# A four-layer WKV and graph-convolution kernel: both ends rearranged, three groups of rows for 1/std, maxima of three tiles per operation, square of means from PSUM

## The chip, the cores and the metric

The kernel runs on one core of a Trainium2 chip. The core has five engines, each with its own stream of instructions: TensorE (PE in the profile; its weight loads are shown as PEld) multiplies matrices into PSUM, VectorE (DVE) does arithmetic between tensors, ScalarE (ACT) does functions of one operand, GpSimd (POOL) does arithmetic between tensors too, and SyncE (SP) issues most transfers. They meet at semaphores. The metric is the time of one execution on the device in microseconds.

## What is computed

The input x has 16 images of 192 channels and 56 x 56 points in float32. Three layers of one kind and a fourth of another kind follow each other, each adding to x what it computes from the group-normalized x:

```python
def rwkv(x):                      # layers 0, 1, 2, on tokens t = 0..3135
    k, v, r = x @ Wk.T, x @ Wv.T, x @ Wr.T
    h = sigmoid(r) * 0.5 * (wkv_scan(w, u, k, v) + flip(wkv_scan(w, u, flip(k), flip(v))))
    h = (h - mean(h)) * rsqrt(var(h) + 1e-5) * ln_g + ln_b      # over the 192 channels
    return h @ Wo.T
def graph_conv(x):                # layer 3
    xj = maximum(0, roll(x, +-2, rows) - x, roll(x, +-2, columns) - x)
    return gelu(batch_norm(concat(x, xj) @ conv_w.T + conv_b))
for l in range(3):
    x = x + rwkv(group_norm(x))   # 32 groups of 6 channels, over all points
x = x + graph_conv(group_norm(x))
```

The scan is a recurrence over tokens with a decay for each channel; it runs forward and backward, so that a layer needs all tokens of an image before its backward half ends, and the group norm needs all of them before the next layer begins.

## The kernel before

**Tiling.** Images go in eight pairs. The 384 channels of a pair lie in three tiles of 128 rows: j = 0 has channels 0 to 127 of the first image, j = 2 those of the second, and the middle tile j = 1 has the last 64 channels of both, the first image's in rows 0 to 63 (LO in the code), the second's in rows 64 to 127 (HI). The 3136 tokens are cut into NL = 7 chunks of L = 448, eight rows of the image each. All x and h tiles are 128 x 3 x 448, so one operation over all three j has 1344 elements in a row.

**Runs and units.** A run is one layer of one pair: 8 x 4 runs. A run of layers 0 to 2 has seven A units (keys, values, forward scan of a chunk; a_keys to a_y) and seven B units, from chunk 6 down to 0 (backward scan, gate, norm over channels, output projection, residual; b_gate to b_stats). A run of layer 3 has seven C units (c_rows to c_add). Chunks of x go through DRAM between the runs (b_x stores, load_chunk loads).

**Steps.** Two chains of pairs run against each other: while one pair is in its backward half, the other is in its forward half or its convolution. The list of steps (L1215 to L1270) pairs units: 102 steps have a B and an A unit, 66 an A alone, 42 a B and a C, 24 a B alone, 14 a C alone, one none. The order of every engine's instructions is the order in which the step functions (both_a, both_a_first, both_c, forward_a, forward_c, backward_alone) call the parts; the whole of it stands under manual_schedule (L1707), so no scheduler moves anything.

**Norm.** The group norm isn't applied to x. Sums and sums of squares of each chunk are taken on ACT (chunk_stats, L730 to L735: an Identity and a Square for each of the three j, each with an accumulated output into `junk`). For the eight first-layer runs they are taken from the input (Z units); for later layers in b_stats. norm_sums (L738) reduces them on DVE (L740) and multiplies by a group matrix into the PSUM bank psg; norm_var (L746) makes nm, the negative mean, its square m2 (L751), the variance (L753) and 1/std; norm_fold multiplies the weights by it. The mean is carried as one more column of the chunk's tile (mean_column, L764), which a projection turns into a bias. For a run of layer 3 that column sits in chunk 0, so its product has L + 1 columns (c_product, L1131) and gives the bias that c_gelu (L1140) uses for all chunks. For the very first run, all seven chunks are loaded and `count` takes their statistics (L1712, L1713) before anything else of the run.

**1/std of the norm over channels.** For each chunk of a B unit: b_squares (ACT, L1040) squares h; b_sums (PE, L1047, L1049) puts into one bank `st` four bands of 32 rows, two with sums and two with sums of squares, one of each for the two images; b_rs1 (ACT, L1055) and b_rs2 (PE, L1059) subtract the squared mean. b_rs3 then makes 1/std as exp(-0.5 ln) in rows 64 to 127 of the tile `rs`, the first image's in rows 64 to 95, the second's in 96 to 127. b_spread (PE, L1071) copies them by a product with the selection matrix `pick` onto the rows of the three tiles: six instructions, two for each j, with 32 rows of `rs` for j = 0 and 2 and 64 rows for j = 1. b_scale (DVE, L1076) multiplies h by it, b_out (PE, L598 to L607, tile ops) projects, and b_x (DVE, L1089) adds to x. The weight operand is called `fpicks` in the profile. The core of it:

```python
        S.activation(rs[HI, :], st[HI, :L], AF.Ln, bias=eps4[HI, :])      # b_rs3, L1063
        release(st)
        S.activation(rs[HI, :], rs[HI, :], AF.Exp, scale=-0.5)            # L1065
...
        for j, rows in ((0, slice(64, 96)), (2, slice(96, P)), (1, HI)):  # b_spread, L1070
            PE.matmul(ps[j][:, :L], pick[rows, j, :], rs[rows, :], start=True, stop=True)
```

**Convolution.** c_rows (L1108) takes the maximum of the two row neighbours: most of a chunk from the chunk itself (L1114), the first and the last two image rows against 112 tokens of the chunk before and after, which were loaded into the tile (L1115, L1116). c_columns (L1118) takes the column neighbours for each j with one large operation and two for the edges (L1125, L1126, L1127), then the maximum with x (L1128) and with the row maxima (L1129). c_product multiplies x (half 0) and the maxima (half 1) into the same banks (cv), c_gelu applies bias, scale and gelu on ACT (L1150; the gelu needs another table of functions, L1155 loads the first back), c_add adds x on POOL (L1159), and store() sends a unit's result in four transfers one step later.

**The end.** Step 239 is the last with a B unit: chunk 0 of pair 7's layer 2, beside chunk 5 of pair 6's convolution. Steps 240 and 241 have that convolution's chunk 6 and nothing else new, and steps 242 to 248 the seven C units of pair 7 in the order 0 to 6. After the schedule a flag is set on DVE from all the checks of value ranges; where a check fails, a general path (L75 to L470) computes everything again. It isn't taken here.

Of the kernel before, what the change touches and what calls it, by code (L numbers as in the profile page):

```python
# [34 lines left out]
F32 = mybir.dt.float32  # L35
# [438 lines left out]
def fast_path(ctx: ExitStack, tc: tile.TileContext, flag, x, wproj, wfold, wcfold, wconst, wgroup, sums, picks, vecs, out):  # L474
# [237 lines left out]
    class Run:  # L712
        def __init__(self, pr, l, stats, src=None, first=None):
            self.pr, self.l, self.stats, self.src = pr, l, stats, src
            self.xa, self.xb, self.xz = {}, {}, {}
            if first is not None:
                self.xa[0] = first
            self.begun, self.before = False, None
            self.bias, self.ps = {}, {}
            self.ek, self.ekv, self.h, self.den, self.sg, self.rs = {}, {}, {}, {}, {}, {}  # L720
            self.m, self.ml, self.q, self.p = {}, {}, {}, {}
            self.done = set()
# [23 lines left out]
    def norm_var(run):  # L746
        m = run.ps["g"][:, 0:6].rearrange("p (j s) -> p j s", s=2)
        nm = run.nm = stile("nm")
        V.tensor_scalar(nm, m[:, :, 0:1], -1.0 / T, None, ALU.mult)
        m2 = stile("m2")  # L750
        V.tensor_mul(m2, nm, nm)  # L751
        var = run.var = stile("var")
        V.scalar_tensor_tensor(var, m[:, :, 1:2], 1.0 / T, m2, ALU.mult, ALU.subtract)  # L753
        release(run.ps.pop("g"))
        V.tensor_scalar(var, var, EPS, None, ALU.add)
        rstd = run.rstd = stile("rstd")
        S.activation(rstd, var, AF.Ln)
        S.activation(rstd, rstd, AF.Exp, scale=-0.5)
        run.chk = small.tile([P, NCHK], F32, tag="chk", name=name("chk"))
        mean_check = run.chk[:, 3 * NL + 9 : NCHK].rearrange("p (j o) -> p j o", o=1)  # L760
        V.scalar_tensor_tensor(mean_check, var, -MEAN_MAX, m2, ALU.mult, ALU.add)
        mean_column(run, run.xa[0])
# [47 lines left out]
    def load_weights(run):  # L810
        kv = wpool.tile([P, 2, FCOLS], F32, tag="kv", name=name("wkv"))
        if run.l == NLAYERS:
            nc.sync.dma_start(kv, wcfold)
            run.weights = kv, None
        else:
            nc.sync.dma_start(kv, wfold[run.l, :, 0:2, :])
            r = wpool.tile([P, 1, FCOLS], F32, tag="r", name=name("wr"))
            nc.sync.dma_start(r, wfold[run.l, :, 2:3, :])
            run.weights = kv, r
        load_ahead(("C" if run.l == NLAYERS else "A", run, 0))  # L820
# [14 lines left out]
    def load_ahead(unit):  # L835
# [7 lines left out]
        if kind == "C" and c not in run.xb:  # L843
# [217 lines left out]
    def b_rs3(run, c):  # L1061
        rs, st = run.rs[c], run.ps["st"]
        S.activation(rs[HI, :], st[HI, :L], AF.Ln, bias=eps4[HI, :])  # L1063
        release(st)
        S.activation(rs[HI, :], rs[HI, :], AF.Exp, scale=-0.5)  # L1065

    def b_spread(run, c):
        rs = run.rs.pop(c)
        ps = run.ps["rsb"] = banks("rsb")
        for j, rows in ((0, slice(64, 96)), (2, slice(96, P)), (1, HI)):  # L1070
            PE.matmul(ps[j][:, :L], pick[rows, j, :], rs[rows, :], start=True, stop=True)  # L1071
# [36 lines left out]
    def c_rows(run, c):  # L1108
# [3 lines left out]
        if c == 0:  # L1112
            mean_column(run, m)
        V.tensor_max(m.t[:, :, SHIFT:E], xt[:, :, 0 : E - SHIFT], xt[:, :, 2 * SHIFT : L])  # L1114
        V.tensor_max(m.t[:, :, 0:SHIFT], m.t[:, :, 0:SHIFT], xt[:, :, SHIFT : 2 * SHIFT])  # L1115
        V.tensor_max(m.t[:, :, E:L], xt[:, :, E - SHIFT : E], m.t[:, :, E:L])  # L1116

    def c_columns(run, c):  # L1118
# [3 lines left out]
        for j in ORDER:  # L1122
            xr = xt[:, j, :].rearrange("p (r w) -> p r w", w=W)
            mr = ml.t[:, j, :].rearrange("p (r w) -> p r w", w=W)
            V.tensor_max(mr[:, :, 2 : W - 2], xr[:, :, 0 : W - 4], xr[:, :, 4:W])  # L1125
            V.tensor_max(mr[:, :, 0:2], xr[:, :, W - 2 : W], xr[:, :, 2:4])  # L1126
            V.tensor_max(mr[:, :, W - 2 : W], xr[:, :, W - 4 : W - 2], xr[:, :, 0:2])  # L1127
        V.tensor_max(ml.t, ml.t, xt)  # L1128
        V.tensor_max(m, m, ml.t)  # L1129

    def c_product(run, c, half):  # L1131
        n = L + 1 if c == 0 else L
# [7 lines left out]
    def c_gelu(run, c, more):  # L1140
        g, ps = run.ml[c], run.ps["c"]
        if c == 0:
# [22 lines left out]
    def c_end(run, c, more):  # L1165
        c_gelu(run, c, more)
        c_add(run, c)

# [25 lines left out]
    for pr in range(npairs):  # L1194
        runs = [Run(pr, 0, None)]
        for l in range(NLAYERS):
            runs[-1].follow = Run(pr, l + 1, None)
            runs[-1].follow.before = runs[-1]
            runs[-1].dst = [dram.tile([P, 3, L], F32, tag=f"x{pr}_{l}_{c}", name=name("xd")) for c in range(NL)]
            runs.append(runs[-1].follow)  # L1200
# [11 lines left out]
    while ready[turn] is not None:  # L1212
# [16 lines left out]
        if len(streams) == 1 or ready[other] is None:  # L1229
# [8 lines left out]
            else:  # L1238
                ready[turn] = None
            steps += [[None, None, []]] + [[None, u, []] for u in units]  # L1240
# [367 lines left out]
    def forward_c(a, nback, nfront):  # L1608
# [5 lines left out]
        if h and ahead and nfront[0] == "A":  # L1614
# [16 lines left out]
            return  # L1631
        c_product(*a, 0)
        c_rows(*a)
        c_columns(*a)
# [12 lines left out]
        c_end(*a, nfront is not None and nfront[0] == "C")  # L1647
# [58 lines left out]

    with tc.manual_schedule(engines={PE.engine, V.engine, S.engine, G.engine, nc.sync.engine}):  # L1707
        S.preload_act_table_set(TABLES)
        first = chains[0][0]
        for c in range(NL):  # L1710
            load_ahead(("Z", first, c))
        for c in range(NL):  # L1712
            count([(first, c, j) for j in ORDER], 3)  # L1713
        for i, (b, f, z) in enumerate(steps):
# [32 lines left out]
            elif f:  # L1747
                forward_c(f[1:], nback, nfront)
# [7 lines left out]


    least = small.tile([P, 1], F32, tag="p2", name="fleast")
    V.tensor_reduce(least, ok, mybir.AxisListType.X, ALU.min)
    ps = bank("psok")  # L1760

    PE.matmul(ps[0:32, 0:1], ones[:, 0, :], least, start=True, stop=True)
    V.tensor_scalar(flag, ps[0:1, 0:1], (P - 0.5) / C, None, ALU.is_lt)
# [44 lines left out]
def _lay_out(inputs):  # L1808
# [24 lines left out]
    picks[64, 0, :] = picks[64, 1, 0:64] = picks[96, 1, 64:P] = picks[96, 2, :] = 1.0  # L1833
# [22 lines left out]
```

## Time and profile before

| quantity | value |
|---|---|
| median of 3 executions | 5122.39 us (5105.55 to 5124.11) |
| the profiled execution | 5118.31 us |
| its span in the profile | 5116.5 us |
| granted TensorE clock, mean | 0.95 |
| HBM | 324.83 MB read, 154.14 MB written, 94 GB/s |
| the chain that ended last, largest lines | POOL L1033 6%, L1032 6%, L1031 5%; DVE scan L875 p 5%, q 4% |
| largest groups | DVE scans L875, two groups of 1008: 1023.5 and 1020.1 us |

The profile shows one execution. A group of instructions has a line of the kernel, an engine, the tiles it writes and reads, a shape, a count, the busy time and the mean of one, and the idle time of the engine just before, with what ended it. The chain that ended last is followed back from the last instruction: at each step to what released it, or else to the instruction before it on its engine. POOL and DVE durations of one operation differ from one instance to the next where both engines are busy, so undisturbed durations are read from instances with no neighbour. The slices of the page show DVE at 5 tenths in the first slice and 5 in the last, 8 or 9 in almost all others; the first and the last 128 us have less work side by side than the rest.

### The profile page before, as it was taken

How to read it: one execution, taken by the hardware profiler on the slowest of the kernel's cores; microseconds unless marked ns; L12 is line 12 of the kernel's file. 1: busy time of each engine (PE TensorE's matmuls, PEld its weight loads, DVE VectorE, ACT ScalarE, POOL GpSimd, SP SyncE). 2: the span in 40 equal slices, each digit the busy share in tenths (PEclk: the TensorE clock that was granted, in tenths of full speed). 3: DMA queues.
4: the chain of work that ended last, by engine and by line, in shares of the span. 5: the costliest groups of instructions: out<-in, count | busy, mean ns of one | idle time of the engine just before them, and what ended most of it. 6: DMA issues, size and time to landing. Idle time of an engine off the chain costs nothing.

```text
span 5116.5 us, 51926 instructions
## 1 busy us (share of the span) xinstructions
PE 4664.1 (91%) x15542; PEld 1474.9 (29%) x15542; DVE 4769.5 (93%) x6275; ACT 3690.8 (72%) x7163; POOL 2898.8 (57%) x2247
## 2 busy tenths in 40 slices
PE   7899999999898999999989899999989999999897
PEld 3222222222222223222323222322222322223222
DVE  5999999998999999999899999999989999999995
ACT  6777777776767777777776777777767577777672
POOL 1656656654455666565455556666635466566562
PEclk9999999999899999999999999999999999999998
DMA  6122222234242222223424222222343322222233
GB/s 173 60 84 82 80 87 84 79 103 144 79 129 88 85 76 89 78 76 121 138 89 126 79 83 72 89 89 78 114 124 113 103 65 84 78 71 89 74 100 119
DMA packets 314276, 482.49 MB, mean 94 GB/s; under 512 B 66432, under 2 KB 306688, under 8 KB 313984
## 3 DMA queue, kind: packets, MB, share of 16 engines
q1 hardware_dynamic: 312832, 477.59, 29.2%
q8 instruction: 126, 2.06, 0.2%
q10 hardware_dynamic: 1152, 1.48, 0.1%
q14 instruction: 166, 1.36, 0.1%
HBM read 324.83 MB, written 154.14 MB: 94 GB/s over the span
## 4 chain that ended last, share of the span: by engine, by line
PE 35%; DVE 23%; POOL 18%; ACT 17%; issue 4%; DMA 2%; SPq 1%; POOLq 0%; DVEq 0%; ACTq 0%
POOL p L1033 6%; POOL p L1032 6%; POOL ekv L1031 5%; DVE p L875 5%; DVE q L875 4%; PE st L1049 3%; DVE q L890 2%; ACT sg L1003 2%; PE st L1059 2%; ACT sg L978 2%; ACT ek L978 2%; PE rsb L1071 2%; PE r L598 2%; PE r L605 2%; PE r L600 2%
## 5 line engine op out<-in xcount | busy, mean ns | idle before, releaser
L875 DVE TENSOR_TENSOR_SCAN q<-fdecays,ek 128x449 f32<-128x449 f32 (+1 forms) x1008 | 1023.5, 1068 | 12.8 <-ACT ek L920 10.3
L875 DVE TENSOR_TENSOR_SCAN p<-fdecays,ekv 128x449 f32<-128x449 f32 (+1 forms) x1008 | 1020.1, 1064 | 15.1 <-ACT ek L884 14.9
L1031 POOL TENSOR_TENSOR ekv<-ekv,ek 128x448 f32<-128x448 f32 x504 | 609.6, 1210 | 607.6 <-ACT ek L978 284.3
L982 POOL TENSOR_TENSOR p<-p,q 128x1344 f32<-128x1344 f32 x168 | 512.2, 3049 | 749.8 <-ACT q L978 468.6
L1033 POOL TENSOR_TENSOR p<-p,sg 128x448 f32<-128x448 f32 x504 | 616.8, 1224 | 83.4 <-ACT sg L978 34.0
L1032 POOL TENSOR_TENSOR p<-p,ekv 128x448 f32<-128x448 f32 x504 | 602.3, 1195 | 39.5
L886 POOL COPY ekv<-p 128x3 f32<-128x3 f32 x282 | 243.8, 864 | 567.0 <-DVE p L875 544.4
L920 ACT ACTIVATE ek<-k,k 128x448 f32<-128x448 f32 x504 | 297.1, 632 | 285.6 <-PE k L601 229.2
L1040 ACT ACTIVATE ek<-p 128x448 f32<-128x448 f32 x504 | 286.3, 572 | 231.2 <-POOL p L1033 230.8
L735 ACT ACTIVATE fjunk<-x 128x448 f32<-128x448 f32 x672 | 387.7, 577 | 37.6 <-DVE x L1089 11.1
L1071 PE MATMUL rsb<-rs,fpicks 32*128 32x448 f32 (+1 forms) x1008 | 355.3, 619 | 43.1 <-ACT rs L1065 43.1
L1076 DVE TENSOR_TENSOR p<-p,rsb 128x448 f32<-128x448 f32 x504 | 281.4, 611 | 103.7 <-PE rsb L1071 103.7
L890 DVE SCALAR_TENSOR_TENSOR ek<-ek,fcc,q 128x896 f32<-128x896 f32 x336 | 377.7, 1163 | 0.0
L734 ACT ACTIVATE fjunk<-x 128x448 f32<-128x448 f32 x600 | 343.5, 572 | 13.6
L1089 DVE SCALAR_TENSOR_TENSOR x<-ops,fwob,x 128x448 f32<-128x448 f32 x504 | 313.2, 669 | 29.5 <-PE ops L601 16.2
L890 DVE SCALAR_TENSOR_TENSOR q<-ek,fcc,q 128x896 f32<-128x896 f32 x336 | 334.7, 1035 | 6.3 <-ACT cvb L954 4.6
L940 DVE SCALAR_TENSOR_TENSOR ekv<-v,v,ek 128x448 f32<-128x448 f32 x504 | 312.3, 671 | 15.3 <-PE v L601 10.9
L890 DVE SCALAR_TENSOR_TENSOR ekv<-ekv,fcc,p 128x896 f32<-128x896 f32 x336 | 321.7, 997 | 0.0
L996 ACT ACTIVATE sg<-r,r 128x448 f32<-128x448 f32 x504 | 312.4, 626 | 10.2 <-PE r L607 8.3
L890 DVE SCALAR_TENSOR_TENSOR p<-ekv,fcc,p 128x896 f32<-128x896 f32 x336 | 293.6, 913 | 3.8 <-POOL ekv L886 1.7
L975 ACT ACTIVATE q<-q 128x1344 f32<-128x1344 f32 x168 | 221.5, 1318 | 96.9 <-DVE q L890 87.8
L598 PE MATMUL ops<-p,fwo 128*128 128x448 f32 x336 | 206.1, 700 | 84.5 <-DVE p L1076 84.5
(235 smaller groups left out, 11485.2 us busy)
## 6 DMA issues: line engine op xcount, KB each, us to landing
x<-xd SPq DMA_DIRECT2D x240, 672.0 KB, 5.3
xd<-x SPq DMA_DIRECT2D x168, 672.0 KB, 3.9
x<-in_x_dram SPq DMA_DIRECT2D x320, 224.0 KB, 4.5
x<-in_x_dram SPq DMA_DIRECT2D x320, 112.0 KB, 4.4
out_dram<-ml SPq DMA_DIRECT2D x112, 224.0 KB, 2.3
m<-xd SPq DMA_DIRECT2D x112, 168.0 KB, 5.2
wkv<-in_wfold_dram SPq DMA_DIRECT2D x24, 640.0 KB, 5.5
out_dram<-ml SPq DMA_DIRECT2D x112, 112.0 KB, 2.3
```

Of the source, the lines that this page charges most:

```text
L734: S.activation(junk, xt[:, j, :], AF.Identity, accum_out=stats[:, 0, j, c : c + 1])
L735: S.activation(junk, xt[:, j, :], AF.Square, accum_out=stats[:, 1, j, c : c + 1])
L875: V.tensor_tensor_scan(out, dec[:, column(j)].to_broadcast([P, L if first else L + 1]), e, 0.0, ALU.mult, ALU.add)
L890: by_channel(lambda js, i: V.scalar_tensor_tensor(dst.t[:, js, :], e.t[:, js, :], cc[:, i : i + 1], state.t[:, js, :], ALU.mult, ALU.add))
L940: V.scalar_tensor_tensor(e.t[:, j, :], ps[j][:, 0:L], b[:, j, :], run.ek[c].t[:, j, :], ALU.add, ALU.mult)
L982: G.tensor_mul(run.h[c].t, run.h[c].t, den.t)
L996: S.activation(sg.t[:, j, :], ps[j][:, 0:L], AF.Exp, bias=b[:, j, :], scale=-1.0, accum_out=run.chk[:, at : at + 1])
L1031: G.tensor_mul(y.t[:, j, :], y.t[:, j, :], den.t[:, j, :])
L1032: G.tensor_add(h.t[:, j, :], h.t[:, j, :], y.t[:, j, :])
L1033: G.tensor_mul(h.t[:, j, :], h.t[:, j, :], sg.t[:, j, :])
L1071: PE.matmul(ps[j][:, :L], pick[rows, j, :], rs[rows, :], start=True, stop=True)
L1089: V.scalar_tensor_tensor(xj, ps[j][:, 0:L], wob[:, column(j)], xj, ALU.add, ALU.add, accum_out=run.new[:, 0, j, c : c + 1] if c == 0 else ...
```

## The change

It has five parts.

1. The first run's sums are taken on DVE, one reduction for a whole chunk; ACT keeps only the squares.
2. m2 is computed by scalar_tensor_tensor from the mean in PSUM and nm, in place of a product of nm with itself.
3. b_rs3 writes 1/std a second time, into rows 0 to 63 of `rs`, by another Exp. The middle tile's matmul of b_spread takes these rows, and `pick` is laid out for it: 32 rows from 64, 32 from 96, 64 from 0.
4. The two edge operations of c_rows become one over a strided view, and c_columns treats the three tiles together: three operations in place of nine.
5. The last run's C units go in the order 3, 4, 5, 2, 6, 1, 0; unit c0 = 3 carries the mean's column and the bias. The step of the last C unit of the run before is written out anew (`final` in forward_c): the squares of the last backward chunk are issued first, the row and column maxima of unit 3 stand ahead of the scaling on DVE, those of unit 4 ahead of and behind the residual, the second half of the product and the gelu come last. The very last unit goes tile by tile, with gelu, an addition on DVE and the transfers for each tile, and the range flag is set before it. The other steps of the list are unchanged.

```diff
-            self.begun, self.before = False, None
+            self.begun, self.before, self.nm = False, None, None
+
+            self.c0 = 0
...
-        V.tensor_mul(m2, nm, nm)
+        V.scalar_tensor_tensor(m2, m[:, :, 0:1], -1.0 / T, nm, ALU.mult, ALU.mult)
...
-        mean_column(run, run.xa[0])
+        mean_column(run, run.xa[run.c0])
+        if run.c0 in run.m:
+            mean_column(run, run.m[run.c0])
...
         rs, st = run.rs[c], run.ps["st"]
         S.activation(rs[HI, :], st[HI, :L], AF.Ln, bias=eps4[HI, :])
         release(st)
+
+        S.activation(rs[LO, :], rs[HI, :], AF.Exp, scale=-0.5)
         S.activation(rs[HI, :], rs[HI, :], AF.Exp, scale=-0.5)
 
     def b_spread(run, c):
         rs = run.rs.pop(c)
         ps = run.ps["rsb"] = banks("rsb")
-        for j, rows in ((0, slice(64, 96)), (2, slice(96, P)), (1, HI)):
+        for j, rows in ((0, slice(64, 96)), (2, slice(96, P)), (1, LO)):
             PE.matmul(ps[j][:, :L], pick[rows, j, :], rs[rows, :], start=True, stop=True)
...
         xt, m = run.xa[c].t, run.xb.pop(c)
         run.m[c] = m
         E = L - SHIFT
-        if c == 0:
+        if c == run.c0 and run.nm is not None:
             mean_column(run, m)
         V.tensor_max(m.t[:, :, SHIFT:E], xt[:, :, 0 : E - SHIFT], xt[:, :, 2 * SHIFT : L])
-        V.tensor_max(m.t[:, :, 0:SHIFT], m.t[:, :, 0:SHIFT], xt[:, :, SHIFT : 2 * SHIFT])
-        V.tensor_max(m.t[:, :, E:L], xt[:, :, E - SHIFT : E], m.t[:, :, E:L])
+        mq, xq = (t.rearrange("p j (q k) -> p j q k", k=SHIFT) for t in (m.t, xt))
+        V.tensor_max(mq[:, :, ::3], mq[:, :, ::3], xq[:, :, 1:3])
 
...
 
         m, xt, ml = run.m[c].t, run.xa[c].t, Slot("ml")
         run.ml[c] = ml
-        for j in ORDER:
-            xr = xt[:, j, :].rearrange("p (r w) -> p r w", w=W)
-            mr = ml.t[:, j, :].rearrange("p (r w) -> p r w", w=W)
-            V.tensor_max(mr[:, :, 2 : W - 2], xr[:, :, 0 : W - 4], xr[:, :, 4:W])
-            V.tensor_max(mr[:, :, 0:2], xr[:, :, W - 2 : W], xr[:, :, 2:4])
-            V.tensor_max(mr[:, :, W - 2 : W], xr[:, :, W - 4 : W - 2], xr[:, :, 0:2])
+        xr, mr = (t.rearrange("p j (r w) -> p j r w", w=W) for t in (xt, ml.t))
+        V.tensor_max(mr[:, :, :, 2 : W - 2], xr[:, :, :, 0 : W - 4], xr[:, :, :, 4:W])
+        V.tensor_max(mr[:, :, :, 0:2], xr[:, :, :, W - 2 : W], xr[:, :, :, 2:4])
+        V.tensor_max(mr[:, :, :, W - 2 : W], xr[:, :, :, W - 4 : W - 2], xr[:, :, :, 0:2])
         V.tensor_max(ml.t, ml.t, xt)
         V.tensor_max(m, m, ml.t)
 
+    def maxima(run, c):
+        if c not in run.ml:
+            c_rows(run, c)
+            c_columns(run, c)
+
...
+    def c_end_in_parts(run, c):
+
+        g, ps, xs = run.ml.pop(c), run.ps["c"], run.xa.pop(c)
+        b0, b1 = 2 * run.pr, 2 * run.pr + 1
+        cols = slice(c * L, (c + 1) * L)
+        for j in ORDER:
+            S.activation(
+                g.t[:, j, :], ps[j][:, 0:L], AF.Gelu, bias=run.bias["c"][:, j, :], scale=conv_inv[:, column(j)]
+            )
+            release(ps[j])
+            V.tensor_add(g.t[:, j, :], g.t[:, j, :], xs.t[:, j, :])
+            if j == 1:
+                nc.sync.dma_start(out[b0, P:C, cols], g.t[LO, 1, :])
+                nc.sync.dma_start(out[b1, P:C, cols], g.t[HI, 1, :])
+            else:
+                nc.sync.dma_start(out[(b0, b1)[j // 2], 0:P, cols], g.t[:, j, :])
+        g.give()
+        xs.give()
+
...
+            if units[0][0] == "C":
+
+                last = units[0][1]
+                last.c0 = 3
+                units = [("C", last, c) for c in (3, 4, 5, 2, 6, 1, 0)]
...
+        l0, l2 = of_stage(0), of_stage(2)
+        if l0 and final:
+
+            r3, r4 = (u[1:] for u in final[:2])
+            load_ahead(final[0])
+            b_squares(*l0)
+            c_product(*a, 0)
+            c_rows(*a)
+            c_columns(*a)
+            store()
+            b_sums(*l0)
+            load_ahead(final[1])
+            if l2:
+                add(l2)
+            b_rs1(*l0)
+            b_rs2(*l0)
+            b_rs3(*l0)
+            b_spread(*l0)
+            sum_up()
+            maxima(*r3)
+            b_scale(*l0)
+            b_out(*l0)
+            c_rows(*r4)
+            add(l0)
+            sum_up()
+            c_product(*a, 1)
+            gap()
+            gap()
+            c_columns(*r4)
+            gap()
+            gap()
+            c_gelu(*a, True)
+            c_add(*a)
+            return
         c_product(*a, 0)
-        c_rows(*a)
-        c_columns(*a)
+        maxima(*a)
...
+        if nfront is None:
+            flag_up()
+            c_end_in_parts(*a)
+            return
+        c_end(*a, nfront[0] == "C")
...
+    def flag_up():
+
+        least = small.tile([P, 1], F32, tag="p2", name="fleast")
+        V.tensor_reduce(least, ok, mybir.AxisListType.X, ALU.min)
+        ps = bank("psok")
+
+        PE.matmul(ps[0:32, 0:1], ones[:, 0, :], least, start=True, stop=True)
+        V.tensor_scalar(flag, ps[0:1, 0:1], (P - 0.5) / C, None, ALU.is_lt)
+        release(ps)
...
+        first.stats = input_stats()
         for c in range(NL):
-            count([(first, c, j) for j in ORDER], 3)
+            xs = first.xz.pop(c)
+            V.tensor_reduce(first.stats[:, 0, :, c : c + 1], xs.t, mybir.AxisListType.X, ALU.add)
+            chunk_stats(first.stats, xs.t, c, True)
+            xs.give()
...
-    picks[64, 0, :] = picks[64, 1, 0:64] = picks[96, 1, 64:P] = picks[96, 2, :] = 1.0
+    picks[64, 0, :] = picks[0, 1, 0:64] = picks[32, 1, 64:P] = picks[96, 2, :] = 1.0
```

## The prediction

> **What bounds the kernel now.** I read the page first, then the chain of waits, then the groups by line and shape, then the timeline of single steps.
>
> ```profile
> span 5116.5 us, 51926 instructions
> ...
> PE 4664.1 (91%) x15542; PEld 1474.9 (29%) x15542; DVE 4769.5 (93%) x6275; ACT 3690.8 (72%) x7163; POOL 2898.8 (57%) x2247
> ...
> PE 35%; DVE 23%; POOL 18%; ACT 17%; issue 4%; DMA 2%; SPq 1%; POOLq 0%; DVEq 0%; ACTq 0%
> ```
>
> The first row gives the span, the second the busy time of each engine, the third each engine's share of the chain that ended last. No engine is the bound alone: DVE and PE are nearly full, yet POOL and ACT carry a third of the chain. One step of the main loop is a ring: ACT prepares a quotient, POOL multiplies it, ACT squares, PE sums, ACT makes 1/std, PE spreads it, DVE scales, PE projects. So one microsecond taken from an engine is worth what the chain shows at that line, not its whole busy time.
>
> The groups by line and shape, for the lines that the change touches (busy and mean ns, then idle time before them and who ended it):
>
> ```profile
> L1065 ACT ACTIVATE rs<-rs 64x448 f32<-64x448 f32 x168 | 96.3, 573 | 5.4
> L1003 ACT ACTIVATE sg<-sg 128x1344 f32<-128x1344 f32 x168 | 222.5, 1324 | 2.3
> L1071 PE MATMUL rsb<-rs,fpicks 64*128 64x448 f32 x336 | 189.8, 648 | 0.0
> L1071 PE MATMUL rsb<-rs,fpicks 32*128 32x448 f32 x672 | 177.3, 604 | 43.1 <-ACT rs L1065 43.1
> L751 DVE TENSOR_TENSOR m<-nm 128x3 f32<-128x3 f32 x32 | 37.5, 1171 | 1.1
> L753 DVE SCALAR_TENSOR_TENSOR var<-psg,m 128x3 f32<-128x3 f32 x32 | 5.1, 160 | 1.1
> L1115 DVE TENSOR_TENSOR m<-m,x 128x336 f32<-128x336 f32 x56 | 61.1, 1090 | 0.0
> L1116 DVE TENSOR_TENSOR m<-x,m 128x336 f32<-128x336 f32 x56 | 52.5, 938 | 0.0
> L1125 DVE TENSOR_TENSOR ml<-x 128x416 f32<-128x416 f32 x168 | 99.4, 591 | 24.4 <-ACT ml L1150 10.3 <-PE st L1049 9.7 <-DMA out_dram<-ml 3.4
> ```
>
> The reader is to see three things: 1/std (L1065) is followed by work that never waits (L1003, idle 2.3 us in 168); L751 squares three numbers in 1171 ns where its neighbour L753 needs 160; and the small maxima are long for their size.
>
> **Start.** Before the first fold, ACT takes sum and square of 7 x 3 tiles, 42 operations at a pitch of 0.70 us. By the timeline DVE waits for the last of them:
>
> ```profile
> 49.51 0.20 DVE L740 TENSOR_REDUCE mv<-zstats 128x6 f32<-128x42 f32 x1 [16.32 <-ACT fjunk L735]
> ```
>
> Afterwards ACT has 21 squares. One is done before 21.5 us (parameter work lies between), so 20 x 0.70 end at about 35.5. DVE gets 7 reductions of 128x1344; the nearest row is L1128, the same elements, 1.57 us undisturbed. Four can lie in DVE's gaps before 33.2 us, three follow: 33.2 + 3 x 1.57 = 37.9. DVE becomes the last, and the wait ends 49.5 - 37.9 = 11.6 us earlier. Between a free reduction (35.5, 14.0) and one at twice the price (42.6, 6.9) I take **-11.6**. The loads don't hold it: their issues for this stage end at 22.0, about 5.5 us from landing.
>
> **Square of the mean.** 32 operations. 20 take 0.16 us, 12 take about 2.7: L751 reads two operands in SBUF and stands behind a POOL operation; L753, which reads PSUM, never does. The new one reads PSUM too, so DVE saves (1171 - 160) x 32 = 32.4 us. On the chain L751 has 22.5 us in 24 pieces; without 24 x 0.16 = 3.8 that leaves **-19** (ends 0 and -32: it may stand at the next two-operand operation instead).
>
> **Maxima.** The two edge operations (L1115, L1116) become one; nine column operations become three. Undisturbed pitches: edges 0.42 + 0.42 to about 0.77; columns 3 x 0.67 = 2.01 to about 1.61, if the cost per element stays and each operation dropped saves its fixed part (16 elements cost 0.08 us of pitch). That is 0.47 us per unit, x 56 = 26 us. Further, means of 1090 and 938 ns against 500 undisturbed say that each operation may wait for POOL anew; one lock fewer per unit is worth up to 0.4 us, 22 us in all. DVE saves 26 to 48. Of 56 units the chain has about 20 in the rows (L1115 18.9, L1116 11.8 us) and 26 in the columns (L1125 to L1127, 58 us), so near half: (26 + 22) / 2 = **-24** (ends -8 and -40).
>
> **Spread.** The second Exp adds 168 x 0.573 = 96 us on ACT, same shape as the L1065 row. It lies between L1065 and the sigmoid's L1003, which follows within 24 ns in 92 of 168 cases (the activation table load in 35 more), so it pushes the backlog; POOL's product then starts later, because it waits for ACT (L1031). L1065 itself is on the chain 95 times, 54.5 us. A delay put into a chain piece is a delay of the end, so I take **+54** (ends: +30, where ACT has idle time before its next due operation, as 1.8 us at 1009 us; +96, all on the path). Cover exists only where PE is still at a projection: the spread starts a median 3.0 us after L1065, and at once in 32 cases.
>
> What does it buy? The middle tile's matmul moves from rows 64-127 to rows 0-63, so that its rows no longer overlap those of the two others. If all three ran together the spread would fall from 1.91 to 0.95 us: -0.95 x 168 = -160 us of PE. The weight loads of one spread:
>
> ```profile
> 1006.96 0.30 PEld L1071 LDWEIGHTS rsb<-rs,fpicks 32*128 32x128 f32 x4 [0.71 <-ACT sg L1003]
> 1007.91 0.29 PEld L1071 LDWEIGHTS rsb<-rs,fpicks 64*128 64x128 f32 x2 [0.65 <-issue]
> ```
>
> The 64-row load waits 0.65 us with nothing named, until the 32-row pair has passed. I find the same 0.65 us at each change of tile size (128*128 to 128*64 too) against 0.19 us where the size stays. But in every such place the rows also overlap, so the trace can't say which of the two ends the wait. Two rules stand here. The Trainium skill, "TensorE: Matmul & The Clock Gate" (table under "Why this matters for your kernels"), lets matmuls in distinct groups of rows run at once; by it -160 us on PE, and on the chain, where the spread has 89.2 us, about half of it, -45. The skill's "TensorEngine Tiling (Array Packing)", section Key Properties, speaks against the change: changing the mode, not just the tile, drains TensorE, and 32 rows beside 64 is a change of mode. By it the gain is nothing, and +54 stays. The first rule is stated for tiles of one size, and no pair of different sizes runs at once anywhere in this trace, so I take **0** for PE (other end -45, and -80 if DVE's waits of 103.7 us for the spread go too).
>
> **End.** Before, the last backward chunk's squares stand on ACT behind the gelu of the convolution unit before it and 12 statistics operations, and DVE waits for their result (rows of ACT, then of DVE):
>
> ```profile
> 5003.97 0.19 ACT L735 ACTIVATION_READ_ACCUMULATOR fjunk<-x 128x1 f32 x1
> 5004.06 1.49 ACT L1040 ACTIVATE ek<-p 128x448 f32<-128x448 f32 x3
> ...
> 5012.31 1.15 DVE L1076 TENSOR_TENSOR p<-p,rsb 128x448 f32<-128x448 f32 x2 [22.79 <-PE rsb L1071]
> ```
>
> After, the squares go first (about 4976), 1/std is ready at 4988. Now c_rows and c_columns of unit 3 are queued on DVE ahead of the scaling (about 6 us), so scaling runs from about 4994 and x is done at 5001 against 5021.7. The folded weights' load (5.84 us), the fold and the first product follow at 5015 against 5029.7: -14.7. The stretch from there to the last product was 74.7 us, with holes of about 9 us (5.5 of them at 5045); two units' maxima are ready beforehand, so I count 65: product ends at 5080 against 5104.4, -24. The last unit goes tile by tile, DVE's add of 0.66 in place of POOL's 3.02 at 5105: -3 to -4, with SP's last four issues unchanged in number. Sum **-28** (ends -18 and -34). Chunk order changes what SP loads, not how much.
>
> **Sum.** -11.6 - 19 - 24 + 54 + 0 - 28 = -29 against the profiled execution's 5118.3: **5090**. The three times shown have a median of 5122.4 and spread over 18.6 us, so the profiled one is a fair base.
>
> **Rivals.**
> *The three groups do run together.* For: separate rows, separate banks. Against: the 0.65 us at changes of size. -29 - 45 = -74: 5044.
> *ACT becomes the bound in the loop (slower side).* Place: the queue behind b_rs3. Price: 0.573 us each time. For: the following operation never waits (2.3 us over 168). Against: ACT is 72% busy and idle elsewhere. At all 168, and with half the DVE gains eaten by waits for ACT: +96 - 21 - 11.6 - 28 = +35: 5154. It decides from 84 us on, that is when 146 of 168 lie on the path with all other gains kept, or about 107 (61 us) with half of the DVE gains kept.
> *The ends alone.* The loop's gains and losses cancel: -40, 5079; it lies in the first case's range.
>
> **How the numbers follow.** Forecast (no overlap) 0.54, own range 5065 to 5120; overlap 0.27, 5015 to 5070; slower side 0.19, 5120 to 5165. The range 5035 to 5140 leaves out the bottom of the second and the top of the third. 0.5% is about what a measurement of this kernel can tell from no change: faster is below 5097, slower above 5148. Faster: two thirds of the first case and all of the second, 0.61; slower: half of the third and a little of the first, 0.13; same 0.26.
>
> **What would show it.** Start: L740 at 38 instead of 49.5. Square: L751's mean at 160 to 200 ns. Maxima: DVE's group total of L1114 to L1129 falling from 560 us by 26 to 48. Spread: whether the 64*128 rows of L1071 start at the same time as the 32*128 rows, and how often ACT's second Exp lies on the chain. End: DVE's 22.8 us before the last scaling gone, and the last product ending some 24 us nearer to that point. I would be wrong if the loop between 60 and 4960 us grew by over 60 us or shrank by over 40.

## The result and the profile after

The changed kernel takes 5118.48 us in the median of 12 runs (5116.23 to 5120.04), the kernel before 5118.82 on the same chip (5094.06 to 5124.11); the ratio is 1.0008, with a 95% interval from 0.9996 to 1.002. So there is no change that can be measured, where 29 us less were forecast. The runs of the kernel before fall into two groups here, five of 5094 to 5108 us and seven of 5118 to 5124 with the profiled one (5118.31) near the latter, while on the chip of experiment 1 its 57 runs lie around 5107. So a difference of a few us to the single profile of before means nothing by itself.

The page of the changed kernel, for the rows shown of before:

```profile
span 5117.6 us, 51804 instructions
...
PE 4657.8 (91%) x15542; PEld 1479.2 (29%) x15542; DVE 4779.8 (93%) x5893; ACT 3768.5 (74%) x7286; POOL 2905.9 (57%) x2246
...
PE 40%; DVE 19%; ACT 17%; POOL 17%; issue 5%; DMA 1%; SPq 1%; DVEq 0%; POOLq 0%; ACTq 0%
```

DVE has 382 instructions fewer and yet 10 us more busy time; ACT has 78 us more. The granted TensorE clock (the share of its full rate that the profile shows TensorE was given) is 0.954 in the mean, against 0.950 before. The groups by line and shape:

```profile
L1070 ACT ACTIVATE rs<-rs 64x448 f32<-64x448 f32 x168 | 96.7, 575 | 5.3
L1071 ACT ACTIVATE rs<-rs 64x448 f32<-64x448 f32 x168 | 96.3, 573 | 5.3
L753 DVE SCALAR_TENSOR_TENSOR m<-psg,nm 128x3 f32<-128x3 f32 x32 | 5.1, 161 | 1.1
L757 DVE TENSOR_SCALAR var<-var 128x3 f32<-128x3 f32 x32 | 26.8, 839 | 1.1
L1129 DVE TENSOR_TENSOR ml<-x 128x1248 f32<-128x1248 f32 x56 | 102.0, 1822 | 27.9 <-PE st L1053 11.8 <-DMA out_dram<-ml 7.0 <-ACT ml L1159 7.0
L1122 DVE TENSOR_TENSOR m<-m,x 128x672 f32<-128x672 f32 x56 | 96.6, 1726 | 2.0 <-DMA m<-xd 2.0
```

L1070 is the second Exp. The square (L753) now takes 161 ns as forecast, and the operation two rows on, the addition of eps (L757, 169 ns before), 839. The seven groups of maxima (L1120 to L1133), of which two are shown, sum to 494 us, against 560 in eight groups before: 66 us less, more than the 26 to 48 forecast.

**Where it came and went.** The forward and backward scans are 2016 operations in the same order in both kernels. Their starts in the two traces, changed kernel minus before:

| place (time in the kernel before) | difference, us |
|---|---|
| first scan (63 us) | -11.4 |
| 876 us | -4.2 |
| 2085 us | +1.6 |
| 3085 us | +13.9 |
| 4088 us | +17.3 |
| last scan (4950 us) | +24.3 |
| end | +1.1 |

The start wins 11.4, the end 23.2, and the loop between loses 35.7. To see where the loop loses, I took the time from each b_rs3 to the next in both traces, by the kind of the two steps: 85 pairs of steps with a B and an A unit lose 0.37 us each (31.6 in all), 34 pairs with B and C units lose 0.31 each (10.7), and the stretches with an A unit alone win 0.56 each (17 of them, 9.6). Two theories stand: the second Exp is what it costs (theory 1), or DVE's and POOL's new order does it (theory 2).

### The profile page after: what moved, and what is told of

Read it like the earlier page. It is cut to its first block, busy times and chain, and to the rows that moved or that the text cites. A ratio compares the mean times of both kernels' runs of the same rounds, so it can differ in the third digit from the quotient of the medians.

```text
span 5117.6 us, 51804 instructions
## 1 busy us (share of the span) xinstructions
PE 4657.8 (91%) x15542; PEld 1479.2 (29%) x15542; DVE 4779.8 (93%) x5893; ACT 3768.5 (74%) x7286; POOL 2905.9 (57%) x2246
## 3 DMA queue, kind: packets, MB, share of 16 engines
q8 instruction: 126, 2.06, 0.2%
## 4 chain that ended last, share of the span: by engine, by line
PE 40%; DVE 19%; ACT 17%; POOL 17%; issue 5%; DMA 1%; SPq 1%; DVEq 0%; POOLq 0%; ACTq 0%
POOL p L1037 5%; POOL p L1036 5%; POOL ekv L1035 5%; DVE q L879 4%; DVE p L879 4%; PE st L1053 3%; PE rsb L1077 2%; DVE q L894 2%; DVE ekv L944 2%; PE st L1063 2%; ACT ek L982 2%; PE r L598 2%; PE r L605 2%; PE r L600 2%; PE v L598 2%
## 5 line engine op out<-in xcount | busy, mean ns | idle before, releaser
L1077 PE MATMUL rsb<-rs,fpicks 32*128 32x448 f32 (+1 forms) x1008 | 371.5, 626 | 62.7 <-ACT rs L1071 62.7
L737 ACT ACTIVATE fjunk<-x 128x448 f32<-128x448 f32 x672 | 387.6, 577 | 31.8 <-issue 8.5
L894 DVE SCALAR_TENSOR_TENSOR ek<-ek,fcc,q 128x896 f32<-128x896 f32 x336 | 377.1, 1161 | 0.0
L894 DVE SCALAR_TENSOR_TENSOR q<-ek,fcc,q 128x896 f32<-128x896 f32 x336 | 358.5, 1106 | 6.3 <-ACT cvb L958 4.7
L736 ACT ACTIVATE fjunk<-x 128x448 f32<-128x448 f32 x579 | 331.5, 573 | 13.0
L894 DVE SCALAR_TENSOR_TENSOR ekv<-ekv,fcc,p 128x896 f32<-128x896 f32 x336 | 323.0, 1001 | 0.0
L894 DVE SCALAR_TENSOR_TENSOR p<-ekv,fcc,p 128x896 f32<-128x896 f32 x336 | 297.4, 924 | 3.4 <-POOL ekv L890 1.7
L1059 ACT ACTIVATE rs<-st 64x448 f32<-64x448 f32 x168 | 90.0, 536 | 227.9 <-PE st L1053 226.6
```

The costliest lines, as they stand in the source:

```text
L736: S.activation(junk, xt[:, j, :], AF.Identity, accum_out=stats[:, 0, j, c : c + 1])
L737: S.activation(junk, xt[:, j, :], AF.Square, accum_out=stats[:, 1, j, c : c + 1])
L894: by_channel(lambda js, i: V.scalar_tensor_tensor(dst.t[:, js, :], e.t[:, js, :], cc[:, i : i + 1], state.t[:, js, :], ALU.mult, ALU.add))
```

## The experiments

The lines of an edit are against the changed kernel, where not said otherwise. Ratios are to the kernel before on the same chip, with 95% intervals; us are worked out from them with its median there (5107 to 5119). Experiments 5, 7, 8 and the first part of 9 ran on another chip than the rest.

**1. The spread of before, the rest changed.**

```diff
-        S.activation(rs[LO, :], rs[HI, :], AF.Exp, scale=-0.5)
-        for j, rows in ((0, slice(64, 96)), (2, slice(96, P)), (1, LO)):
+        for j, rows in ((0, slice(64, 96)), (2, slice(96, P)), (1, HI)):
-    picks[64, 0, :] = picks[0, 1, 0:64] = picks[32, 1, 64:P] = picks[96, 2, :] = 1.0
+    picks[64, 0, :] = picks[64, 1, 0:64] = picks[96, 1, 64:P] = picks[96, 2, :] = 1.0
```

> The changed kernel with its third part undone: one Exp, the middle tile's matmul reads rows 64 to 127 again. Theory 1 (the second Exp delays ACT's queue by 0.573 us in each of 168 steps, of which the step lengths of the two traces show about 0.37 in a step with a B and an A unit, and the matmuls run one after the other with either layout): about 48 us less than the changed kernel, near 5070. Theory 2 (the second Exp is mostly hidden, and what was lost in the loop comes from the new order of DVE's and POOL's operations by the parts 2 and 4): 0 to 15 us less, near 5110.

5065.85 us, ratio 0.9924 [0.991, 0.9937]. The same kernel a second time, beside those of experiments 6, 9 and 10:

> The first experiment's kernel a second time, beside the other three on one chip: 0.9924 of the kernel before, between 0.991 and 0.994.

5065.29 us, ratio 0.9914 [0.99, 0.9927]. Theory 1 holds. In the profile of the first of the two the B and A pairs differ from those of before by 0.01 us each.

**2. The new spread alone, in the kernel before** (the reverse of the edit of experiment 1).

> The kernel before with the third part alone: second Exp and the new rows for the middle tile. Theory 1: 45 to 55 us above the kernel before, near 5168. Theory 2: 0 to 15 us above, near 5127.

5164.59 us, ratio 1.0117 [1.0102, 1.0133]: +60 [52, 68]. Here the B and A pairs lose 0.38 each, as in the changed kernel. The third part alone is the loop's loss.

**3. The second Exp kept, its rows not read** (the edit of experiment 1 without its first line; the Exp's result is left unused).

> The changed kernel, with the second Exp kept but its rows 0 to 63 not read: the middle tile's matmul reads rows 64 to 127 as before. If the rows of the matmuls have no effect at all on PE (a change of tile size drains it either way), the time is that of the changed kernel, 5118 within 5. If the free rows win something that the trace hides, it is slower than the changed kernel by that, up to 40.

5118.27 us, ratio 1.0022 [1.0015, 1.003], against 1.0008 [0.9996, 1.002] of the changed kernel. The rows that the middle tile's matmul reads have no effect; the price is the Exp's alone, 1.0022 - 0.9924 = 0.98%, 50 us, on the chip of experiment 1.

**4, 5, 6. Parts alone, in the kernel before.** Parts 2 and 4 together, part 2, part 4 (their lines of the diff, nothing else):

> The kernel before with parts 2 and 4 alone: the mean's square from PSUM, merged maxima. Theory 1: 8 to 15 us below the kernel before, near 5107, because of DVE's 66 us less in the maxima the step lengths of the two traces show nearly nothing where a convolution runs. The prediction's sum: 43 us below, near 5076. Theory 2: above the kernel before by 15 to 25, near 5138.

> The kernel before with the square of the mean read from PSUM and nothing else. If the wait goes away with its instruction, as the prediction had it: 19 us below the kernel before (0.9963). If DVE meets the same wait at the next operation that has only SBUF operands (the trace of the changed kernel shows the addition of eps at 839 ns in the mean, 32 times): 0 to 6 us below (0.9988 to 1.0000).

> The kernel before with the merged maxima alone. By the prediction: 24 us below the kernel before (0.9953). By the step lengths of the runs so far: nothing in the loop, because there DVE waits elsewhere for POOL and ACT, and about 8 us at the end, where the last convolution units stand alone: 0.9985.

Both: 5095.56 us, ratio 0.9982 [0.9976, 0.9989], -9 us [-12, -6]. The square alone: 5104.62, 0.9977 [0.9964, 0.9991], -12 [-18, -5]. The maxima alone: 5099.27, 0.9984 [0.9976, 0.9991], -8 [-12, -5]. The two together show no more than either. The reason lies with the square's figure. On its chip the kernel before has ten runs with a granted clock of 0.951 or more, 5103.2 us in the mean, and fifteen with 0.949 or less, 5121.3. All ten runs of the square's kernel take 5098.5 to 5108.5 us, 5103.9 in the mean, no less than those ten. So the -12 comes from the other fifteen; whether the edit is what spares the kernel such runs is not shown. On the other chip, where the maxima alone and both together ran, the square adds only 1 to 3 us to the maxima (0.9982 against 0.9984; means 5096.8 and 5099.3). So the second expectation, 0 to 6 us, is the nearer one. DVE's rows in the square's kernel alone agree with it:

```profile
L751 DVE SCALAR_TENSOR_TENSOR m<-psg,nm 128x3 f32<-128x3 f32 x32 | 5.1, 161 | 1.1
L755 DVE TENSOR_SCALAR var<-var 128x3 f32<-128x3 f32 x32 | 32.7, 1022 | 1.1
```

The square falls from 37.5 to 5.1 us, and the addition of eps, L755 here, rises from 5.4 to 32.7: of 32.4 us, 5.1 are left. In the profile the square's kernel is 11.7 us shorter in the six stretches between a convolution and the next backward half, where the norm is waited for. But these stretches also hold 22 us less at halved clock (126.0 against 148.4; what halving costs is shown in experiment 8), which by an estimate at half speed is worth up to 11 of them. How much the square itself wins there stays open.

How the wait moves is seen in one step, the same one in three kernels. Timeline rows of DVE, before:

```profile
1437.60 2.81 DVE L751 TENSOR_TENSOR m<-nm 128x3 f32<-128x3 f32 x1
```

and after:

```profile
1436.41 0.16 DVE L753 SCALAR_TENSOR_TENSOR m<-psg,nm 128x3 f32<-128x3 f32 x1
1436.60 0.16 DVE L755 SCALAR_TENSOR_TENSOR var<-psg,m 128x3 f32<-128x3 f32 x1
1436.80 2.46 DVE L757 TENSOR_SCALAR var<-var 128x3 f32<-128x3 f32 x1
```

The two that read PSUM pass in 0.16 us, and the first operation that has only SBUF operands waits out the rest. What it waits for in this step is POOL's addition of the convolution unit, before:

```profile
1436.97 3.42 POOL L1159 TENSOR_TENSOR ml<-ml,x 128x1344 f32<-128x1344 f32 x1
```

The Trainium skill's "SBUF — State Buffer", section "SBUF: two separate sides", says that the pair of ports which DVE and POOL share is locked for a whole instruction, and names operations of DVE with two SBUF inputs and those in a two-port mode. The 0.16 against 2.46 and 2.81 us agree; that L757, which reads one tensor, ran in such a mode is not shown.

Why the maxima win almost nothing in the loop is seen in one step with a B and a C unit. Timeline rows of POOL, before, then with the merged maxima alone (the step that begins with b_rs3's Ln at 1417.29 and 1415.31 us):

```profile
1425.14 1.45 POOL L1031 TENSOR_TENSOR ekv<-ekv,ek 128x448 f32<-128x448 f32 x1 [7.21 <-ACT sg L996]
1426.67 1.14 POOL L1032 TENSOR_TENSOR p<-p,ekv 128x448 f32<-128x448 f32 x1
1427.89 1.14 POOL L1033 TENSOR_TENSOR p<-p,sg 128x448 f32<-128x448 f32 x1
```

```profile
1422.69 1.46 POOL L1031 TENSOR_TENSOR ekv<-ekv,ek 128x448 f32<-128x448 f32 x1 [6.72 <-DVE ekv L890]
1424.22 1.14 POOL L1032 TENSOR_TENSOR p<-p,ekv 128x448 f32<-128x448 f32 x1
1425.81 1.14 POOL L1033 TENSOR_TENSOR p<-p,sg 128x448 f32<-128x448 f32 x1 [0.44 <-ACT sg L978]
```

POOL begins its first product 0.47 us sooner after the step's begin, because DVE is done sooner. But its third product needs the gate's Exp from ACT, which stands behind the gelu and two table loads and is not sooner; POOL waits 0.44, and only 0.1 us is left of the gain. In the 34 B and C pairs together 5.1 us are won, 0.15 a pair; 3.3 of them lie in the two pairs in which the trace of before has a stretch of halved clock (one begins with the step shown), so 1.8 in the other 32. About 8 us are won in the last 150 us of the run, where no B unit runs beside.

**7. The ends alone, in the kernel before** (parts 1 and 5).

> The kernel before with the parts 1 and 5 alone: sums on DVE at the start, the end in its new order. The traces of the changed kernel and of the first experiment show 11.4 us at the start and 23 to 24 us at the end: 35 below the kernel before (0.9932). If the end's part there came from the merged maxima and not from the order: 25 below or less (0.9950).

5079.65 us, ratio 0.9925 [0.9905, 0.9945], -38 [-49, -28]. The interval is too wide to tell the two expectations apart; the profiles speak for the second: from the last b_rs3 interval to the end this kernel wins 16.6 us, the one of experiment 1, with the merged maxima, 24.6. With 11.4 at the start that is 28.0, and the four runs of this kernel with a clock of 0.953 or more (mean 5075.2; the two others have 0.949 and 5097.6) are 28 us below the runs of before with 0.951 or more.

**8. A third Exp** (the added line of part 3 twice; it computes the same).

> The changed kernel with the second Exp written twice, so that ACT has three Exps in each step. If the price of an Exp is what it pushes the queue behind it, the third costs as much as the second, about 52 us above the changed kernel: near 5170 (1.0100). If ACT still had idle time to hide part of the second, the third costs more, 70 to 96: near 5200. If the second's price came from its place in front of the spread and not from ACT's time, it would cost under 30.

5322.80 us, ratio 1.0397 [1.0381, 1.0413]. It was expected at 52 to 96 us above the changed kernel and is 204 above, more than twice what the operation itself takes (168 x 0.573 = 96). No theory had this. The B and A pairs lose 1.78 us each on top, 151 in all. Two things happen in them. The first is a collision. Rows of POOL and DVE in one such step of the changed kernel, and in the same step with three Exps:

```profile
948.03 1.13 POOL L1037 TENSOR_TENSOR p<-p,sg 128x448 f32<-128x448 f32 x1
948.75 1.96 DVE L894 SCALAR_TENSOR_TENSOR q<-ek,fcc,q 128x896 f32<-128x896 f32 x2
```

```profile
990.67 2.06 POOL L1037 TENSOR_TENSOR p<-p,sg 128x448 f32<-128x448 f32 x1
990.61 2.60 DVE L894 SCALAR_TENSOR_TENSOR q<-ek,fcc,q 128x896 f32<-128x896 f32 x2
```

In the changed kernel POOL's last product of the step is at work before DVE comes to the bonus (L894). Half a microsecond later they collide: DVE's operation starts first, POOL's takes 2.06 instead of 1.13 us. PE's last sums wait for that product, r's projection stands behind them in PE's queue, and ACT's gate waits for r. PE's wait at this place over the run (idle before L1053):

```profile
L1053 PE MATMUL st<-p,fsums 128*32 128x448 f32 x672 | 159.2, 552 | 96.5 <-POOL p L1037 96.5
```

```profile
L1053 PE MATMUL st<-p,fsums 128*32 128x448 f32 x672 | 181.9, 623 | 207.2 <-POOL p L1037 207.1
```

It was 54.7 us in the kernel before: each Exp is handed on to it, and the third one more than in full.

The second thing is the clock. PE's rows in the same step, of the changed kernel, then with three Exps:

```profile
949.22 0.95 PE L1053 MATMUL st<-p,fsums 128*32 128x448 f32 x4 [0.90 <-POOL p L1037]
950.70 1.02 PE L598 MATMUL r<-x,wr 128*128 128x448 f32 x2
```

```profile
992.78 0.95 PE L1053 MATMUL st<-p,fsums 128*32 128x448 f32 x4 [2.42 <-POOL p L1037]
994.66 1.86 PE L598 MATMUL r<-x,wr 128*128 128x448 f32 x2
```

PE's wait has grown from 0.90 to 2.42 us, by the Exp (0.57) and POOL's longer product (0.93). About a microsecond after PE resumes, the granted clock is halved for 3.41 us, and r's first product takes 1.86 instead of 1.02 us. In 68 of the 85 B and A pairs the clock is never halved in the changed kernel; with three Exps 62 of these 68 have a stretch of halved clock. The six others let the costs be told apart. Three such stretches, from b_rs3 to b_rs3, with three Exps (from and to, length, busy time of the engines, granted clock as PEclk):

```profile
core 0: us, PE busy (x) PEld busy (x) DVE busy (x) ACT busy (x) POOL busy (x), PEclk, DMA share, GB/s
1769.53:1792.04 22.51, 20.38 (x70) 6.21 (x70) 19.80 (x25) 18.24 (x33) 11.92 (x11) 1.00 0.23 78
566.09:591.77 25.68, 23.26 (x81) 7.12 (x82) 24.33 (x29) 20.29 (x39) 18.63 (x16) 1.00 0.24 81
974.09:1001.42 27.33, 24.91 (x81) 7.61 (x82) 24.95 (x30) 20.39 (x39) 15.99 (x13) 0.94 0.21 76
```

The same steps of the changed kernel take 21.90, 24.15 and 24.16 us. The first has no collision (POOL's product takes 1.13 us) and loses 0.6 us, what the Exp takes. The second has the collision at full clock, as four more pairs have, and loses 1.5. The third has both and loses 3.2; the 62 pairs with halved clock lose 2.8 in the mean. So of the 182 us that the 68 pairs lose, about 41 are the Exp's own, 62 the collision's and 79 go with the clock. (The 17 other pairs, with halved clock in both kernels, win 30 back.) Over the run the halved clock takes 724 us in place of 471, and the mean clock is 0.930 to 0.933 in the five runs, against 0.953 to 0.956 in the twelve of the changed kernel. The five pairs with the collision at full clock have the same wait of 2.42 us, so the wait alone does not decide it; what else does is not shown.

**9. Tiles of one size.** Six products of 32 rows by 64 columns:

```diff
-        for j, rows in ((0, slice(64, 96)), (2, slice(96, P)), (1, LO)):
-            PE.matmul(ps[j][:, :L], pick[rows, j, :], rs[rows, :], start=True, stop=True)
+        q2, q3 = slice(64, 96), slice(96, P)
+        for j, rows, out in ((0, q2, LO), (0, q2, HI), (2, q3, LO), (2, q3, HI), (1, slice(0, 32), LO), (1, slice(32, 64), HI)):
+            PE.matmul(ps[j][out, :L], pick[rows, j, out], rs[rows, :], start=True, stop=True)
```

> The changed kernel with the spread written in six products of 32 rows by 64 columns in place of three of 32 or 64 rows by 128: rows 64 to 95 onto both halves of tile 0, 96 to 127 onto both halves of tile 2, 0 to 31 and 32 to 63 onto the two halves of the middle tile. All have one tile size and no two share rows and columns. If the change of tile size is what drained PE: the six run together, the spread takes 0.95 instead of 1.97 us, and the time falls by 30 to 60 below the changed kernel, 5060 to 5090. If PE doesn't overlap them for another reason: the spread takes 2 us or more, and the time is that of the changed kernel or above, 5118 to 5200.

5107.37 us, ratio 0.9984 [0.9973, 0.9996]: 12 us below the changed kernel. The timeline of PE, of one spread in the changed kernel and in this one (weight loads, then matmuls):

```profile
1005.14 0.30 PEld L1077 LDWEIGHTS rsb<-rs,fpicks 32*128 32x128 f32 x4 [0.71 <-issue]
1006.09 0.29 PEld L1077 LDWEIGHTS rsb<-rs,fpicks 64*128 64x128 f32 x2 [0.65 <-issue]
...
1005.14 1.97 PE L1077 MATMUL rsb<-rs,fpicks 32*128 32x448 f32 x6
```

```profile
1005.11 0.22 PEld L1078 LDWEIGHTS rsb<-rs,fpicks 32*64 32x64 f32 x12 [0.70 <-issue]
...
1005.12 0.99 PE L1078 MATMUL rsb<-rs,fpicks 32*64 32x448 f32 x12
```

With sizes mixed, the 64-row loads wait 0.65 us and the spread takes 1.97, as in the kernel before (1006.96 us there), although no rows overlap any more. With one size all six run at once in 0.99. PE is busy 172 us less in this run (4485.9 against 4657.8), and the time falls by 12, which is not the 30 to 60 expected. PE only gets to its next wait sooner: the projection's wait for the scaling on DVE grows from 62.0 to 179.9 us.

The same with one Exp, on top of experiment 1, where the middle tile must read rows 64 to 127 and so follow in a second round:

> The first experiment's kernel (changed kernel, one Exp) with the spread in products of 32 rows by 64 columns: rows 64 to 95 onto both halves of tile 0 and the lower half of the middle tile, 96 to 127 onto both halves of tile 2 and the upper half of the middle tile. Two of the six share their rows and columns with one of the others, so they must follow: two rounds, about 1.9 us as before, but without a change of tile size inside the spread. Expected: the time of the first experiment within 8 us, 0.9924 of the kernel before. If PE's time in the spread is what counts in the steps with an A unit: no gain either. If the change of size inside it cost time on the path: 5 to 15 us below the first experiment.

5059.30 us, ratio 0.99 [0.9885, 0.9915], against 0.9914 [0.99, 0.9927] of experiment 1's kernel in the same set: not told apart. PE's busy time in all spreads is 316.2 us here, against 186.9 with six separate tiles: at one size, products that share rows and columns still take a second round. Either kernel is faster than the kernel before, by 44 and 51 us.

**10. More work for DVE.** The kernel of parts 2 and 4 alone, with the last maximum of each convolution unit written twice:

```diff
         V.tensor_max(m, m, ml.t)
+        V.tensor_max(m, m, ml.t)
```

> The fourth experiment's kernel (mean's square from PSUM, merged maxima) with the last maximum of each convolution unit written twice: 56 more operations of about 1.6 us, 90 us of DVE, which change no value. If DVE's time in a convolution unit is off the path in the loop: 11 us for the last seven units, and up to 15 in the rest, so 10 to 25 above the fourth experiment (1.0005 to 1.003 of the kernel before). If half of it lies on the path, as the prediction had it for what the maxima save: 45 above (1.007). If all: 90 (1.016).

5143.06 us, ratio 1.0069 [1.0055, 1.0083], 0.87% or 44 us above that kernel, for 90 us of DVE. The number is the one that the chain's share of a half gives, but the traces of the two kernels show another make-up. The 34 B and C pairs lose 27.3 us. Of these, 22.1 lie in seven pairs that now contain a stretch of halved clock (34 us together, none in the kernel without the repeat); the 27 others lose 5.1 together, for 43 us of DVE (an estimate, 27 x 1.6). The last 157 us of the run lose 6.7, and most of the rest lies in stretches that also gain time at halved clock. So at full clock the addition is mostly hidden too, as the saving was, and the half is luck.

## Why the prediction was wrong

By its steps, in us:

| step | forecast | measured |
|---|---|---|
| start | -11.6 | -11.4 (first scan, traces) |
| square of the mean | -19 | -12 [-18, -5], no less than before's runs at a clock of 0.951 or more; -1 to -3 beside the maxima |
| maxima | -24 | -8 [-12, -5] |
| both together | -43 | -9 [-12, -6] |
| second Exp | +54 | +50 (experiment 3 minus 1); +60 [52, 68] alone |
| overlap in the spread | 0 | 0 |
| end | -28 | -23.2 (traces) |
| sum | -29 | +4 [-2, +10] |

**What failed is the square and the maxima**: together 34 us short, where the sum missed by 33; the rest, 5 at the end and 4 at the Exp, has both signs. The step was, in the prediction's words, "Of 56 units the chain has about 20 in the rows [...] and 26 in the columns [...], so near half: (26 + 22) / 2", and for the square, "On the chain L751 has 22.5 us in 24 pieces". DVE's saving in the maxima was even larger than taken (66 us). But the chain tells which wait ended last, not by how much. In the step shown, ACT's gate was only 0.1 us behind DVE; after that tenth the saving went into POOL's wait for ACT. What the prediction asked of others, "where a stall goes, what is late next", it didn't ask here. The wait of the square was followed too short: it had been bounded by "it may stand at the next two-operand operation instead", and it went to the next operation with SBUF operands alone, the addition of eps, which took over 27.3 of the 32.4 us. The measured steps add up to +6, the whole to +4. The prediction has no term for the granted clock either, and experiments 8 and 10 show that it can carry a large part of a difference.

**Start** was right in place and size: the DVE reductions end at 37.4 us, the last three directly behind the parameter work; ACT doesn't hold them.

**The second Exp** was right, +54 against +50 to +60, and for the reason given: it stands in ACT's queue between 1/std and what POOL needs. In most B and A steps it costs its whole pitch, as 23.56 to 24.16 us in one of them. The close size is partly luck. Against the trace of experiment 1, the 68 B and A and 34 B and C pairs lose 58 us, all at full clock, and other places 14. The 17 other B and A pairs and the 17 stretches with an A unit alone give 20 back, and in them the time at halved clock falls by 35 us; at half speed that would be up to 17 of the 20 (an estimate).

**No overlap** was right. The question that the trace of before left open, rows or size, is settled by experiments 3 and 9: with mixed sizes separate rows change nothing, and with one size they do. The first is what the skill's "TensorEngine Tiling (Array Packing)" states under Key Properties for a change of mode, and the other rule, of groups of rows that run at once, holds within one size (six in 0.99 us). The prediction's price for an overlap, -45, was too high in the same way as for the maxima: experiment 9 has it, with 172 us less of PE, at -12.

**End.** The gain up to the first product was forecast at 14.7; by the traces it is 14.8 (5039.23 against 5029.74 us, on top of the 24.3 of the loop). The last unit was the mis-sized term: 3 to 4 forecast, 2.4 measured, and the last products were nearer by 21 rather than 24. And a third of it hangs on the merged maxima: 16.6 without them, by experiment 7's profile. DVE's 22.8 us before the last scaling are gone, as said.

**The base**, 5118.3, was called fair; it lies 11 us above the 5107 of the kernel before on the chip of experiment 1.

The rival that ACT becomes the bound had the place and price nearly right (61 us "with half of the DVE gains kept" decides from there), but its time, 5154, needed 96 us for the Exp. Its other threshold, 84 us or 146 steps, is a slip of the sum: the gains of 11.6, 43 and 28 make 82.6 us, or 144 steps. Experiment 8 shows that there was little room left: a third Exp goes beyond it.

## What to carry to other kernels

In a kernel whose steps are a ring through several engines, a saving on a line of the chain is worth only the distance to what is late next, and that has to be looked up at a few places before a share of it is counted. An addition is paid in full where nothing has room behind it (the second Exp, 0.6 us a step) and is mostly hidden where something has (the repeated maximum at full clock). It can cost several times itself when it makes two engines collide and PE wait so long that its clock is halved in most steps; so compare the granted clock before putting a difference of two runs down to an instruction. Before making a product overlap by moving its rows, see whether its tiles have one size; and before paying another engine for it, see whether anyone waits for the product. Undo the parts of a bundled change one by one: here four parts win 39 us together and the fifth gives all of it back.

## What the runs showed of the hardware that was not expected

A third Exp of 0.573 us in each of 168 steps cost 204 us where the second had cost 50. In the steps where it made PE wait 2.42 instead of 0.90 us, the granted clock was halved for 3.4 to 5 us in 62 of 67 pairs and the step grew by 2.8 us in the mean; with the wait of 0.90 the clock was never halved there. Twelve matmul passes of 32 rows by 64 columns took 0.99 us together, as long as four of 32 by 128 (0.95), and the same data in two sizes took 1.97.
